# A four-layer graph network on one core: the first layer in two stages with four sets of rows, the second layer's additions behind the next block's weights

## The chip, the cores and the metric

The kernel runs on one core of one Trainium2 chip. The metric is device time in microseconds (us) of one execution, as the median of several; lower is better. Engines are named as the profile names them: PE is TensorE (matmuls; PEld its weight loads), DVE is VectorE, ACT is ScalarE, POOL is GpSimd, SP is SyncE.

## The reference

6250 nodes with 128 features pass through four layers on one graph. After each layer comes `x = layernorm(x + layer(x))`. The edges are 50,000 random pairs in both directions and one loop per node, 106,250 in all, sorted by destination. Only the first two layers matter here:

```python
# layer 0: attention, 4 heads of 32
xp = (x @ W).reshape(n, HEADS, OUT_C)
e = a_src[src] + a_dst[dst]                 # per edge and head
e = where(e >= 0, e, 0.2 * e)
m = segment_max(e, dst)
ex = exp(e - m[dst])
out = segment_sum(ex * xp[src], dst) / segment_sum(ex, dst) + bias
return relu(out)

# layer 1: weighted differences
theta = x[dst] - x[src]
w = sigmoid(relu(theta @ W1 + b1) @ W2 + b2)
agg = segment_sum(w * theta, dst)
return agg + indeg * (x @ W4 + b4)
```

Both have the same shape of work: for each edge, fetch the row of its source (gather), make a weight from source and destination, and add the weighted rows up per destination. The third layer is a linear attention with a graph convolution, the fourth a sum over neighbours with two dense layers.

## The kernel before, in words

**Tiles.** The nodes are cut into NB = 50 blocks of BN = 125. The edges that end in one block fill at most P = 128 partitions x CE = 18 slots, in order of destination. `dl` holds each slot's destination within its block, `e_all` its source row. FEW = 2 blocks make a pair; some work is done once per pair.

**Order.** The program is written as loops in Python; a scheduler then gives each engine its own order of instructions, with semaphores between engines, and pools of buffers (`bufs=3`: three sets) decide when a buffer may be filled again. Where the source wants a fixed order on one engine without a wait, it adds a dependency by hand: `in_order(inst, ahead)` puts `inst` behind `ahead`, and `follow(inst, b)` puts it behind the last weight of block `b` (`behind_of[b]`). Each engine works through its own order strictly: an instruction that waits holds up all behind it.

**First layer, `quick_layer0`, per block `b`:**

- GpSimd issues 18 indirect gathers into `rows` (L828), one per slot column, 128 rows of `table` each. `rows` has three sets, so the gathers of a block can start when the block three earlier has been summed.
- SP loads `dr`, the destinations of all slots broadcast over 125 partitions; VectorE compares it with the lane number (L844), which makes it a one-hot matrix. With it, 18 bf16 matmuls (L848) fetch each slot's destination terms, `pieces`, into `own_ps`.
- VectorE makes the one-hot `m` of 128 x 2250 in one instruction (L851, 2.5 us).
- The maximum per destination: `side` and `off` (L856 to L861), `each` and `top` (within a partition), `sh_ps` (L870: small shifted matmuls that carry maxima over neighbouring partitions), then `near`, `carry`, `far`, `top`, `z` (L873 to L889).
- The exponent (L891, ScalarE), its copy into `rows` (L892), and the product of all rows with it (L896, VectorE, 2.55 us).
- `gathered` (L341): 18 products `m` x `rows` in float32, 36 matmuls in the trace, summed in one PSUM tile. When this sum is done, `rows` and `m` are free.
- One block later, `to_acc` copies the sum into `acc` (L819, ScalarE). After the second block of a pair, `finish` (L783 to L811) divides, adds the bias and the residual, `norm_few` (L360 to L370) normalizes into `X`, and `table1` (L917 to L929) makes and stores the pair's rows for the next layer.
- In between lie the counting of edges per pair of blocks (`count`) and `sort_keys`, in the first 18 pairs and at blocks 0 and 8. They serve the later layers.

After the loop two copies take the columns `indeg` and `selfs` out of `acc`.

**Second layer, `quick_layer1`, per block `b`:**

- 18 gathers (L1012) into one of the three sets `rows_of`: for each edge the source's `x @ W1` and its `x`.
- `dr` as above (L1016, L1017); 54 bf16 matmuls (L1025) lay the destination's `x @ W1 + b1`, split into three bf16 `parts`, out per slot in five PSUM tiles `theta`; VectorE subtracts the gathered part (L1026) and makes relu times `W2`, summed (`junk`, L1029).
- `gw`, the sigmoid (L1039, ScalarE), and `mw`, the one-hot with the weight in it: 18 instructions on VectorE (L1042), one set.
- `gathered` (L341): `mw` x the rows' `x` part.
- `own` for block `b + 2` (L960 to L981: its `x @ W1 + b1` as `y`, L974, and its three `parts`; L975 and L976 its share of the result), `turned` for block `b + 3`.
- The addition of the sum to the block's `acc` (L1051). After the second block of a pair, `finish` (L984 to L1003): the layer's result, its statistics and `X` (`norm_few`), `xs` and its store into `table2`, four matmuls of the pair's Gram matrix (`gram_ps`, L1000 and L1002) and the addition of that to `gram` (L1003).

Of the kernel before, what the change touches and what calls it, by code (L numbers as in the profile page):

```python
# [8 lines left out]
F32 = mybir.dt.float32  # L9
# [28 lines left out]
FEW = 2  # L38
# [13 lines left out]
def kernel(ctx: ExitStack, tc: tile.TileContext, a: dict, out: bass.AP):  # L52
# [87 lines left out]
    def flat(t):  # L140
        return t.rearrange("p b f -> p (b f)")
# [585 lines left out]
    def quick_layer0(table):  # L727
        with tc.tile_pool(name="q0", bufs=1) as st, tc.tile_pool(name="q0w", bufs=2) as wk:
# [16 lines left out]
            load_xp(0)  # L745
            acc = st.tile([BN, NB, W0], F32, name="acc")
            nth = st.tile([P, NB, GP], BF16, name="nth")
# [35 lines left out]
            def finish(b0):  # L783
                sl = slice(b0, b0 + FEW)
                own = wk.tile([BN, 2, FEW, HEADS], F32, name="own")
                nc.vector.tensor_tensor(own[:, 0], xp[:, sl, A0:A0 + HEADS], xp[:, sl, M0:M0 + HEADS], op=ALU.add)
                nc.vector.tensor_tensor(own[:, 1], acc[:, sl, M0:M0 + HEADS], xp[:, sl, M0:M0 + HEADS], op=ALU.add)
# [12 lines left out]
                nc.vector.tensor_tensor(r, r, acc[:, sl, :F], op=ALU.add)  # L800
                rden = wk.tile([BN, FEW, HEADS], F32, name="rden")
                nc.vector.tensor_tensor(rden, acc[:, sl, A0:A0 + HEADS], part, op=ALU.add)
                nc.vector.reciprocal(rden, rden)
                nc.vector.tensor_tensor(r.rearrange("p b (h c) -> p (b h) c", h=HEADS),
                                        r.rearrange("p b (h c) -> p (b h) c", h=HEADS),
                                        rden.rearrange("p b h -> p (b h)")[:, :, None].to_broadcast([BN, FEW * HEADS, OC]),
                                        op=ALU.mult)
                nc.vector.tensor_tensor(r, r, bias[:, None, :].to_broadcast([BN, FEW, F]), op=ALU.add)
                nc.vector.scalar_tensor_tensor(flat(r), flat(r), 0.0, flat(X[:, sl, :]), op0=ALU.max, op1=ALU.add)
                norm_few(wk, b0, r, FEW)  # L810
                table1(ps, wk, w1, b0, r)  # L811

            with tc.tile_pool(name="q0_ps", bufs=2, space=PSUM) as ps:
                node_ps = ps.tile([P, BN], F32, name="node_ps", bufs=1)
                nc.scalar.copy(node_ps, node)
                left_over = []

                def to_acc(b, s):
                    nc.scalar.copy(acc[:, b, :], s)  # L819
                    if b % FEW == FEW - 1:  # L820
                        finish(b - FEW + 1)

                for b in range(NB):
                    rows = wk.tile([P, CE, W0], F32, name="rows", bufs=3)
                    nc.scalar.copy(rows[:, :, TW], ones[:, :CE])
                    nc.scalar.copy(rows[:, :, TW + 1], self_e[:, b, :])
                    for g in range(CE):
                        nc.gpsimd.indirect_dma_start(  # L828
                            out=rows[:, g, :TW], out_offset=None, in_=table,
                            in_offset=bass.IndirectOffsetOnAxis(ap=e_all[:, b, g:g + 1], axis=0))  # L830
                    d = dl[:, b, :]

                    dr = wk.tile([BN, P * CE], BF16, name="dr")
                    row_load = nc.sync.dma_start(dr, dl_rows[b // BPE][b % BPE:b % BPE + 1, :].to_broadcast([BN, P * CE]))
# [7 lines left out]
                    if b % 2 and b // 2 + 1 < NB // BPE:  # L842
                        split_terms(b // 2 + 1)
                    nc.vector.tensor_scalar(dr, dr, lane[:BN], None, op0=ALU.is_equal)  # L844
                    dr_g = dr.rearrange("d (p g) -> d g p", g=CE)
                    own_ps = ps.tile([P, CE, 6 * HEADS], F32, name="own_ps", bufs=1)
                    for g in range(CE):
                        nc.tensor.matmul(own_ps[:, g, :], dr_g[:, g, :], pieces[:, b].rearrange("p q s -> p (q s)"),  # L848
                                         start=True, stop=True)
                    m = wk.tile([P, CE, BN], F32, name="m")  # L850
                    nc.vector.tensor_tensor(m, node_ps[:, None, :].to_broadcast([P, CE, BN]),  # L851
                                            d[:, :, None].to_broadcast([P, CE, BN]), op=ALU.is_equal)

                    off = wk.tile([P, CE, CE], F32, name="off", bufs=1)
                    side = ps.tile([P, 1 + 2 * HEADS, CE], F32, name="side", bufs=1)
                    nc.scalar.copy(side[:, 0, :], d)  # L856
# [12 lines left out]
                    for k in range(2 * SPAN):  # L869
                        nc.tensor.matmul(sh_ps[:, k, :], shift[:, k, :], top[:, :, CE - 1] if k < SPAN else top[:, :, 0],  # L870
                                         start=True, stop=True)
                    own = wk.tile([P, 2 * HEADS, CE], F32, name="own")
                    nc.vector.tensor_reduce(own, own_ps.rearrange("p g (q s) -> p q g s", s=3), axis=AX.X, op=ALU.add)  # L873
# [17 lines left out]
                    nc.scalar.activation(ex, z[:, 0].rearrange("p h g -> p g h"), AF.Exp)  # L891
                    nc.scalar.copy(rows[:, :, A0:A0 + HEADS], ex)  # L892
                    nc.vector.tensor_tensor(rows[:, :, M0:M0 + HEADS].rearrange("p g h -> p h g"), top,
                                            begin[:, b, None, :].to_broadcast([P, HEADS, CE]), op=ALU.mult)
                    msg = rows[:, :, :F].rearrange("p g (h c) -> p g h c", h=HEADS)
                    nc.vector.tensor_tensor(msg, msg, ex[:, :, :, None].to_broadcast([P, CE, HEADS, OC]), op=ALU.mult)  # L896
                    s = gathered(ps, m, rows, W0)
                    for later in left_over:
                        later()
                    left_over = []  # L900
                    if b == 2 * EARLY:
# [3 lines left out]
                        nc.vector.memset(before[0:1, :, 0, :], 0.0)  # L905
                    left_over.append(lambda b=b, s=s: to_acc(b, s))
                    if b == 0:
# [3 lines left out]
                    if b % 2 and b // 2 < EARLY:  # L911
                        left_over.append(count(ps, wk, nth, b // 2))
                for later in left_over:
                    later()
            nc.vector.tensor_copy(indeg, acc[:, :, W0 - 2])
            nc.vector.tensor_copy(selfs, acc[:, :, W0 - 1])

# [13 lines left out]
    def quick_layer1(split=None, besides=None):  # L931

        with tc.tile_pool(name="q1", bufs=1) as st, tc.tile_pool(name="q1w", bufs=2) as wk:
# [11 lines left out]
            with tc.tile_pool(name="q1_ps", bufs=1, space=PSUM) as ps:  # L945
# [18 lines left out]
                def own(b, after):  # L964
# [17 lines left out]
                    y_of[b] = parts  # L982

                def finish(c):  # L984
                    r = acc_of.pop(c)
# [9 lines left out]
                    if split is not None:  # L995
                        split(wk, c * FEW, xs)

                    g_ps = ps.tile([F, F + 1], F32, name="gram_ps")
                    for b in range(c * FEW, (c + 1) * FEW):
                        nc.tensor.matmul(g_ps[:, :F], X[:, b, :], X[:, b, :], start=(b == c * FEW), stop=(b == c * FEW + FEW - 1))  # L1000
                    for b in range(c * FEW, (c + 1) * FEW):
                        nc.tensor.matmul(g_ps[:, F:], X[:, b, :], ones[:BN, 0:1], start=(b == c * FEW), stop=(b == c * FEW + FEW - 1))  # L1002
                    nc.vector.tensor_tensor(gram, gram, g_ps, op=ALU.add)  # L1003

# [4 lines left out]
                for b in range(NB):  # L1009
# [31 lines left out]
                    for g in range(CE):  # L1041
                        last = nc.vector.tensor_scalar(mw[:, g, :], node, dl[:, b, g:g + 1], gw[:, g:g + 1],  # L1042
                                                       op0=ALU.is_equal, op1=ALU.mult)
# [658 lines left out]
```

## Time and profile before

| What | Value |
|---|---|
| Median of 9 runs | 4471.13 us (4433.99 to 4502.01) |
| Profiled execution: its own time | 4439.78 us |
| Its span | 4438.0 us, 46396 instructions |
| Mean granted TensorE clock | 0.7 of full speed |
| PE busy (PEld beside it) | 2439.5 us, 55% (1972.2 us) |
| DVE busy | 2181.1 us, 49% |
| ACT busy | 950.5 us, 21% |
| POOL busy | 2329.9 us, 52% |
| First layer, first to last block | 84 to 1484 us of the span |
| Second layer | 1484 to 3101 us |
| Third and fourth layer | 3101 to 4438 us |

How to read it. The page's slices cut the span in 40 equal parts and give each engine's busy share in tenths. Its groups put together the instructions of one line, engine and shape: count, busy time, the mean of one in ns, and then the idle time of the engine just ahead of them, with what ended it (`<-PE gathered L341`: it ended when that matmul reported; `<-issue`: the engine waited for nothing that the profile shows; `<-remote`: a semaphore whose sender was not found, a DMA among others). The timeline gives instructions in order of time: start, duration, engine, line, operation, and in square brackets the idle time ahead. A table by stretch gives each engine's busy time and number of instructions between two moments.

### The profile page before, as it was taken

Reading aid. Unit: us, or ns where it says so; the run is one execution under the profiler, and the core shown is the slowest. Engines: PE = TensorE matmul, PEld = TensorE weight load, DVE = VectorE, ACT = ScalarE, POOL = GpSimd, SP = SyncE. Lnnn points to the kernel's source line nnn. Section 1 sums busy time; section 2 is a strip of 40 time slices with the busy share of each in tenths; the row PEclk is TensorE's granted clock in tenths of the full one; section 3 lists DMA queues with packets and bytes.
Section 4 is the critical chain, followed back from the end, with each engine's and each line's share of the span. In section 5 each row is a group of like instructions: output and inputs, shape, how many; then the busy total and the mean of one; then the engine's idle time right before and its main releaser. Section 6 shows DMA issues by size and latency. Waiting matters only on the chain.

```text
span 4438.0 us, 46396 instructions
## 1 busy us (share of the span) xinstructions
PE 2439.5 (55%) x16000; PEld 1972.2 (44%) x16000; DVE 2181.1 (49%) x6589; ACT 950.5 (21%) x2088; POOL 2329.9 (52%) x2342
## 2 busy tenths in 40 slices
PE   2255554444444344444444444444578778878877
PEld 2244444444443243434334443434467657734434
DVE  2465555555545444444444444545557667722324
ACT  1011111111111101111111111112344435522224
POOL 4566566666666455565555555553733423075550
PEclk6566566656665566666666666666789989988888
DMA  4442233333332233333333333332323223254441
GB/s 108 93 93 71 68 72 77 78 78 75 76 75 61 79 100 91 97 99 91 96 94 98 89 97 95 98 91 58 96 95 108 99 92 114 108 186 157 156 142 51
DMA packets 187556, 422.00 MB, mean 95 GB/s; under 512 B 52793, under 2 KB 98869, under 8 KB 187301
## 3 DMA queue, kind: packets, MB, share of 16 engines
q0 software_dynamic: 88960, 214.29, 19.9%
q1 hardware_dynamic: 82026, 171.37, 11.1%
q10 hardware_dynamic: 16314, 33.19, 2.1%
q8 instruction: 129, 2.11, 0.2%
q14 instruction: 127, 1.03, 0.1%
HBM read 341.45 MB, written 77.23 MB: 94 GB/s over the span
## 4 chain that ended last, share of the span: by engine, by line
PE 30%; issue 19%; DVE 11%; another core or an unknown queue 4%; ACT 2%; POOL 1%; DMA 1%; DVEq 0%; ACTq 0%; SPq 0%; POOLq 0%
PE acc_ps L1517 7%; PE theta L1025 6%; PE gathered L341 6%; PE acc_ps L1290 3%; DVE mw L1042 3%; DVE hit_d L1273 1%; PE c_ps L1279 1%; DVE load L1220 1%; PE own_ps L972 1%; PE s_ps L1478 1%; DVE hit_s L1270 1%; DVE to L1215 1%; DVE m L1562 1%; PE p L1361 1%
## 5 line engine op out<-in xcount | busy, mean ns | idle before, releaser
L1012 POOL DMA_INDIRECT rows<-table1q,e_all x900 | 875.8, 973 | 698.6 <-PE gathered L341 477.5
L828 POOL DMA_INDIRECT rows<-table0q,e_all x900 | 875.5, 973 | 474.9 <-issue 259.3
L1025 PE MATMUL theta<-parts,dr 125*128 125x128 bf16 x2700 | 347.2, 284 | 524.8 <-issue 521.5
L1025 PEld LDWEIGHTS <-dr 125*128 125x128 bf16 x2700 | 284.9, 156 | 593.4 <-issue 586.6
L341 PE MATMUL gathered<-rows,m 128*125 128x138 f32 x1800 | 357.7, 372 | 259.8 <-DVE rows L896 136.7
L1554 POOL DMA_INDIRECT rows<-table2q,e_all x252 | 284.8, 1130 | 385.9 <-PE pre_ps L1380 246.1
L341 PEld LDWEIGHTS gathered<-rows,m 128*125 128x125 f32 x1800 | 335.3, 270 | 269.8 <-DVE rows L896 143.6
L1554 POOL DMA_INDIRECT rows<-table3q,e_all x252 | 267.2, 1060 | 324.5 <-ACT x L1120 154.0
L1290 PE MATMUL acc_ps<-cs,x 125*128 125x250 bf16 x2700 | 395.1, 280 | 17.2 <-issue 17.1
L341 PE MATMUL gathered<-rows,mw 128*125 128x129 f32 x1800 | 303.5, 345 | 159.4 <-DVE mw L1042 139.4
L1517 PE MATMUL acc_ps<-cs,x 125*128 125x500 bf16 x1350 | 329.4, 396 | 88.8 <-issue 72.5
L341 PEld LDWEIGHTS gathered<-rows,mw 128*125 128x125 f32 x1800 | 294.6, 257 | 164.9 <-DVE mw L1042 141.7
L1280 ACT CAST cs<-c_ps 128x500 bf16<-128x500 f32 x450 | 255.6, 577 | 223.4 <-PE c_ps L1279 131.8
L1290 PEld LDWEIGHTS <-x 125*128 125x128 bf16 x2700 | 270.8, 101 | 66.6 <-issue 25.5
L1042 DVE TENSOR_SCALAR mw<-node,dl,gw 128x125 f32<-128x125 f32 x900 | 249.1, 356 | 54.9 <-issue 52.0
L851 DVE TENSOR_TENSOR m<-node_ps,dl 128x2250 f32<-128x2250 f32 x50 | 125.1, 2501 | 293.7 <-remote 172.3
L1517 PEld LDWEIGHTS <-x 125*128 125x128 bf16 x1350 | 134.0, 100 | 277.6 <-issue 146.5
L1279 PE MATMUL c_ps<-hit_d,hit_s 128*128 128x250 bf16 x900 | 185.6, 285 | 104.4 <-issue 72.5
L1029 DVE SCALAR_TENSOR_TENSOR junk<-theta,W 128x128 f32<-128x128 f32 x900 | 209.1, 286 | 2.9 <-DVE junk L1029 2.9
L848 PE MATMUL own_ps<-pieces,dr 125*128 125x24 bf16 x900 | 62.3, 214 | 233.6 <-DVE own L873 118.2
L870 PE MATMUL sh_ps<-top,shift 128*128 128x4 f32 x600 | 103.8, 278 | 140.8 <-issue 111.9
L1003 DVE TENSOR_TENSOR gram<-gram,gram_ps 128x129 f32<-128x129 f32 x25 | 7.3, 292 | 345.6 <-PE gram_ps L1002 345.6
(364 smaller groups left out, 4007.0 us busy)
## 6 DMA issues: line engine op xcount, KB each, us to landing
dr<-dl_rows SPq DMA_DIRECT2D x100, 562.5 KB
counts<-cs SPq DMA_DIRECT2D x90, 625.0 KB
cs<-counts SPq DMA_DIRECT2D x45, 625.0 KB
cs<-counts ACTq DMA_DIRECT2D x45, 625.0 KB
rows<-table0q,e_all POOLq DMA_INDIRECT x900
rows<-table1q,e_all POOLq DMA_INDIRECT x900
rows<-table2q,e_all POOLq DMA_INDIRECT x252
rows<-table3q,e_all POOLq DMA_INDIRECT x252
```

The costliest lines, as they stand in the source:

```text
L341: nc.tensor.matmul(s, m[:, g, :], rows[:, g, :], start=(g == last_first[0]), stop=(g == last_first[-1]))
L828: nc.gpsimd.indirect_dma_start(out=rows[:, g, :TW], out_offset=None, in_=table, in_offset=bass.IndirectOffsetOnAxis(ap=e_all[:, b, g:g + 1 ...
L851: nc.vector.tensor_tensor(m, node_ps[:, None, :].to_broadcast([P, CE, BN]), d[:, :, None].to_broadcast([P, CE, BN]), op=ALU.is_equal)
L1012: nc.gpsimd.indirect_dma_start(out=rows[:, g, :2 * F], out_offset=None, in_=table1_q, in_offset=bass.IndirectOffsetOnAxis(ap=e_all[:, b, g ...
L1025: nc.tensor.matmul(t[:, j, :], dr_g[:, g0 + j, :], y[:, k, :], start=(k == 0), stop=(k == 2))
L1029: nc.vector.scalar_tensor_tensor(junk, t[:, j, :], 0.0, w2, op0=ALU.max, op1=ALU.mult, accum_out=dot[:, g0 + j:g0 + j + 1])
L1042: last = nc.vector.tensor_scalar(mw[:, g, :], node, dl[:, b, g:g + 1], gw[:, g:g + 1], op0=ALU.is_equal, op1=ALU.mult)
L1279: nc.tensor.matmul(c_ps[:, i, :], hit_s[:, j, :, i], hit_d[:, j, :, i], start=True, stop=True)
L1280: nc.scalar.copy(cs[:, 2 * j:2 * j + 2, :], c_ps)
L1290: nc.tensor.matmul(acc_of[q], x3[:, k * SC + j, i, :], cs[:BN, j, :], start=(k == 0 and j == 0 and i == 0), stop=(k == NB // SC - 1 and j ...
L1517: nc.tensor.matmul(acc[:, :n, :], x3[:, k * SC + j, i, :], cs[:BN, :n, j, :], start=(k == 0 and j == 0 and i == 0), stop=False)
L1554: nc.gpsimd.indirect_dma_start(out=rows[:, g, :], out_offset=None, in_=table, in_offset=bass.IndirectOffsetOnAxis(ap=late_e[:, i, g:g + 1] ...
```

## The change

In the first layer the body of the loop is cut in functions: `gather` (rows, `dr`), `highest` (own terms, maxima, shifted maxima), `weigh` (`m`, weights, the product and the sum) and `step` (what was left over from the block before). The loop now issues `gather(b)`, then `weigh` and `step` of block `b - 1`, then `highest(b)`. `rows` has four sets, `dr` three, `own_ps` and `off` two; `side` gets two places in one PSUM bank that it shares with `node_ps`. The tile `acc` of all 50 blocks is replaced by small ones for a pair (three sets), so that `finish` takes it as an argument and copies `indeg` and `selfs` for each pair. The copy of a sum into `acc` is put, on ScalarE, behind the next block's copy of the exponents.

In the second layer the addition of block `b - 1`'s sum (`add_up`), and with it `finish`, is issued behind the weights of block `b` and ahead of block `b`'s sum. The Gram matmuls of a pair stay in `finish`; the addition of their result to `gram` is kept open until the next pair's `finish` (`add_gram`), and the last one is made after the loop.

```diff
-            acc = st.tile([BN, NB, W0], F32, name="acc")
...
-            def finish(b0):
+            def finish(b0, acc):
...
+                nc.vector.tensor_copy(indeg[:, sl], acc[:, :, W0 - 2])
+                nc.vector.tensor_copy(selfs[:, sl], acc[:, :, W0 - 1])
                 norm_few(wk, b0, r, FEW)
                 table1(ps, wk, w1, b0, r)
...
-                node_ps = ps.tile([P, BN], F32, name="node_ps", bufs=1)
+                n_side = (1 + 2 * HEADS) * CE
+                bank = ps.tile([P, 4 * P], F32, name="bank", bufs=1)
+                node_ps = bank[:, :BN]
+                side_of = [bank[:, BN + k * n_side:BN + (k + 1) * n_side].rearrange("p (h g) -> p h g", g=CE) for k in range(2)]
...
-                def to_acc(b, s):
-                    nc.scalar.copy(acc[:, b, :], s)
+                acc_of, weighed = {}, {}
+
+                def to_acc(b, s, after):
+                    if b % FEW == 0:
+                        acc_of[b // FEW] = wk.tile([BN, FEW, W0], F32, name="acc", bufs=3)
+                    copied = nc.scalar.copy(acc_of[b // FEW][:, b % FEW, :], s)
+                    if after in weighed:
+                        tc.add_manual_dep(copied.ins, weighed[after].ins.name, mybir.DependencyInfo(
+                            mybir.DependencyClass.NoSync, mybir.DependencyReason.DATA), reason="order")
                     if b % FEW == FEW - 1:
-                        finish(b - FEW + 1)
-
-                for b in range(NB):
-                    rows = wk.tile([P, CE, W0], F32, name="rows", bufs=3)
+                        finish(b - FEW + 1, acc_of.pop(b // FEW))
+
+                def gather(b):
+
+                    rows = wk.tile([P, CE, W0], F32, name="rows", bufs=4)
...
-                    dr = wk.tile([BN, P * CE], BF16, name="dr")
+                    dr = wk.tile([BN, P * CE], BF16, name="dr", bufs=3)
...
+                    return rows, dr
+
+                def highest(b, rows, dr):
+
                     nc.vector.tensor_scalar(dr, dr, lane[:BN], None, op0=ALU.is_equal)
...
-                    own_ps = ps.tile([P, CE, 6 * HEADS], F32, name="own_ps", bufs=1)
+                    own_ps = ps.tile([P, CE, 6 * HEADS], F32, name="own_ps")
...
-                    m = wk.tile([P, CE, BN], F32, name="m")
-                    nc.vector.tensor_tensor(m, node_ps[:, None, :].to_broadcast([P, CE, BN]),
-                                            d[:, :, None].to_broadcast([P, CE, BN]), op=ALU.is_equal)
-
-                    off = wk.tile([P, CE, CE], F32, name="off", bufs=1)
-                    side = ps.tile([P, 1 + 2 * HEADS, CE], F32, name="side", bufs=1)
+                    d = dl[:, b, :]
+                    off = wk.tile([P, CE, CE], F32, name="off")
+                    side = side_of[b % 2]
...
+                    return b, rows, own_ps, off, top, sh_ps
+
+                def weigh(b, rows, own_ps, off, top, sh_ps):
+
+                    d = dl[:, b, :]
+                    side = side_of[b % 2]
+                    az = side[:, 1:1 + HEADS, :]
+                    m = wk.tile([P, CE, BN], F32, name="m")
+                    nc.vector.tensor_tensor(m, node_ps[:, None, :].to_broadcast([P, CE, BN]),
+                                            d[:, :, None].to_broadcast([P, CE, BN]), op=ALU.is_equal)
                     own = wk.tile([P, 2 * HEADS, CE], F32, name="own")
...
-                    nc.scalar.copy(rows[:, :, A0:A0 + HEADS], ex)
+                    weighed[b] = nc.scalar.copy(rows[:, :, A0:A0 + HEADS], ex)
...
-                    s = gathered(ps, m, rows, W0)
+                    return gathered(ps, m, rows, W0)
+
+                def step(b, s):
...
-                    left_over.append(lambda b=b, s=s: to_acc(b, s))
+                    left_over.append(lambda: to_acc(b, s, b + 1))
...
+                behind = None
+                for b in range(NB):
+                    rows, dr = gather(b)
+                    if behind is not None:
+                        step(b - 1, weigh(*behind))
+                    behind = highest(b, rows, dr)
+                step(NB - 1, weigh(*behind))
...
-            nc.vector.tensor_copy(indeg, acc[:, :, W0 - 2])
-            nc.vector.tensor_copy(selfs, acc[:, :, W0 - 1])
...
+                open_gram = []
+
+                def add_gram(after=None):
+                    if open_gram:
+                        add = nc.vector.tensor_tensor(gram, gram, open_gram.pop(), op=ALU.add)
+                        if after is not None:
+                            follow(add, after)
+
                 def finish(c):
...
+                    add_gram(2 * c + 2)
                     g_ps = ps.tile([F, F + 1], F32, name="gram_ps")
...
-                    nc.vector.tensor_tensor(gram, gram, g_ps, op=ALU.add)
+                    open_gram.append(g_ps)
+
+                def add_up(b, s, after):
+
+                    at = acc_of[b // FEW][:, b % FEW, :]
+                    follow(nc.vector.tensor_tensor(at, at, s, op=ALU.add), after)
+                    if b % FEW == FEW - 1:
+                        finish(b // FEW)
...
                     behind_of[b] = last
+                    if b:
+                        add_up(b - 1, s, b)
                     s = gathered(ps, mw, rows[:, :, F:], F + 1)
...
-                    at = acc_of[b // FEW][:, b % FEW, :]
-                    nc.vector.tensor_tensor(at, at, s, op=ALU.add)
-                    if b % FEW == FEW - 1:
-                        finish(b // FEW)
+                add_up(NB - 1, s, NB)
+                add_gram()
```

More of the change, by code (lines that the diff above doesn't have):

```diff
@@ L786, in finish @@
                 nc.vector.tensor_tensor(own[:, 0], xp[:, sl, A0:A0 + HEADS], xp[:, sl, M0:M0 + HEADS], op=ALU.add)
-                nc.vector.tensor_tensor(own[:, 1], acc[:, sl, M0:M0 + HEADS], xp[:, sl, M0:M0 + HEADS], op=ALU.add)
+                nc.vector.tensor_tensor(own[:, 1], acc[:, :, M0:M0 + HEADS], xp[:, sl, M0:M0 + HEADS], op=ALU.add)
                 own_f = own.rearrange("p k b h -> p (k b h)")
@@ L799, in finish @@
                                             part[:, j, :, None].to_broadcast(shape[:1] + shape[2:]), op=ALU.mult)
-                nc.vector.tensor_tensor(r, r, acc[:, sl, :F], op=ALU.add)
+                nc.vector.tensor_tensor(r, r, acc[:, :, :F], op=ALU.add)
                 rden = wk.tile([BN, FEW, HEADS], F32, name="rden")
-                nc.vector.tensor_tensor(rden, acc[:, sl, A0:A0 + HEADS], part, op=ALU.add)
+                nc.vector.tensor_tensor(rden, acc[:, :, A0:A0 + HEADS], part, op=ALU.add)
                 nc.vector.reciprocal(rden, rden)
@@ L830, in quick_layer0 @@
                             in_offset=bass.IndirectOffsetOnAxis(ap=e_all[:, b, g:g + 1], axis=0))
-                    d = dl[:, b, :]
-                    dr = wk.tile([BN, P * CE], BF16, name="dr")
+                    dr = wk.tile([BN, P * CE], BF16, name="dr", bufs=3)
                     row_load = nc.sync.dma_start(dr, dl_rows[b // BPE][b % BPE:b % BPE + 1, :].to_broadcast([BN, P * CE]))
@@ L896, in quick_layer0 @@
                     nc.vector.tensor_tensor(msg, msg, ex[:, :, :, None].to_broadcast([P, CE, HEADS, OC]), op=ALU.mult)
-                    s = gathered(ps, m, rows, W0)
+                    return gathered(ps, m, rows, W0)
+                def step(b, s):
+                    nonlocal left_over
                     for later in left_over:
```

## The prediction

> **What bounds the kernel now.** I read the page's slices first: up to slice 28 (about 3100 us) no engine is busy much over 60%, so two stages of waits are in question, not a full engine. The groups of instructions by line then name the two that the change touches: the gathers of the first layer (L828) and the second layer's sum of `gram` (L1003).
>
> ```profile
> L1012 POOL DMA_INDIRECT rows<-table1q,e_all x900 | 875.8, 973 | 698.6 <-PE gathered L341 477.5
> L828 POOL DMA_INDIRECT rows<-table0q,e_all x900 | 875.5, 973 | 474.9 <-issue 259.3
> ...
> L1003 DVE TENSOR_TENSOR gram<-gram,gram_ps 128x129 f32<-128x129 f32 x25 | 7.3, 292 | 345.6 <-PE gram_ps L1002 345.6
> ```
>
> L1003 costs 0.29 us a time, and VectorE stands 345.6 / 25 = 13.8 us before each. GpSimd issues a gather in 0.95 us and the next 0.30 us later, so 18 gathers (a **stream**, one block) last 22.5 us.
>
> Both layers show one behaviour that decides this case. Busy time by stretch, cut where streams begin and where TensorE slows; behind the stretch and its length stand busy us and (x instructions) of PE, PEld, DVE, ACT, POOL, then clock and DMA:
>
> ```profile
> 2202.80:2217.10 14.30, 9.79 (x68) 9.04 (x67) 8.46 (x50) 1.18 (x4) 10.95 (x12) 0.75 0.33 93
> 2217.10:2228.30 11.20, 1.53 (x6) 0.84 (x6) 5.45 (x18) 0.00 (x0) 6.37 (x7) 0.64 0.33 94
> 2231.10:2243.30 12.20, 8.83 (x68) 8.47 (x68) 6.00 (x35) 1.85 (x3) 9.46 (x10) 0.78 0.56 144
> 2243.30:2256.50 13.20, 1.72 (x7) 0.72 (x6) 0.48 (x6) 3.35 (x7) 7.59 (x9) 0.50 0.32 90
> ...
> 920.80:937.60 16.80, 9.34 (x67) 9.13 (x67) 11.66 (x30) 1.52 (x8) 12.79 (x14) 0.52 0.39 87
> 937.60:946.10 8.50, 2.11 (x7) 1.22 (x5) 3.36 (x7) 0.00 (x0) 4.47 (x5) 0.66 0.53 114
> ```
>
> After a stream's start TensorE issues about 67 matmuls, whatever they are, and then **crawls**: 6 or 7 in 8 to 13 us, until some 4 us behind the stream's last gather. VectorE goes on at a reduced pace (18 in 11.2 us, 0.62 us each). Why, the trace does not say; I use it as a rule of this kernel.
>
> What TensorE has issued is also reported late. The first layer, in order of time:
>
> ```profile
> 906.41 6.03 PE L341 MATMUL gathered<-rows,m 128*125 128x138 f32 x36 [4.81 <-DVE rows L896]
> ...
> 916.35 0.95 POOL L828 DMA_INDIRECT rows<-table0q,e_all  x1 [0.30 <-issue]
> ...
> 920.62 0.28 ACT L819 COPY acc<-gathered 125x138 f32<-125x138 f32 x1 [13.19 <-PE sh_ps L870]
> 920.62 2.50 DVE L851 TENSOR_TENSOR m<-node_ps,dl 128x2250 f32<-128x2250 f32 x1 [9.99 <-PE sh_ps L870]
> ...
> 920.85 0.95 POOL L828 DMA_INDIRECT rows<-table0q,e_all  x1 [3.55 <-remote]
> ```
>
> The sum of a block is issued by 912.44, and its three readers start together at 920.6, when the stream that ended at 917.3 is 3.3 us past. The freed rows then start the next stream. So a first-layer block lasts 22.5 + 3.3 = 25.8 us, and the gap is made by the stream itself, not by missing buffers. The second layer, an odd block:
>
> ```profile
> 2246.32 0.31 ACT L1039 ACTIVATE gw<-dot,b 128x18 f32<-128x18 f32 x1
> ...
> 2256.59 1.70 PE L1025 MATMUL theta<-parts,dr 125*128 125x128 bf16 x14 [0.45 <-issue]
> ...
> 2260.25 0.29 DVE L1003 TENSOR_TENSOR gram<-gram,gram_ps 128x129 f32<-128x129 f32 x1 [15.70 <-PE gram_ps L1002]
> ...
> 2262.40 3.40 DVE L1042 TENSOR_SCALAR mw<-node,dl,gw 128x125 f32<-128x125 f32 x13
> ...
> 2265.86 1.44 PE L341 MATMUL gathered<-rows,mw 128*125 128x129 f32 x5 [5.64 <-DVE mw L1042]
> ```
>
> The weights' input `gw` is there at 2246.6, but L1003 stands ahead of the 18 weights of L1042 and waits for matmuls that are behind the crawl. Only then come the weights (5.3 us to 2265.8), the block's sum, and the stream that follows it 1.06 us later. Streams start at 2202.8, 2231.1 and 2266.9: 28.3 us for an even block, 35.8 for an odd one, 64.1 a pair.
>
> **Second layer, part by part.** The wait of L1003 goes, since the sum of one pair is added a pair later. The addition of L1051 (0.29 us, waits for its block's sum; 248.3 us idle ahead of it in all, 45 times) moves behind the next block's weights. Late next is the end of the theta matmuls: crawl ends at 2256.6, they last 1.7 us, so the next sum can start at 2258.3 in place of 2265.9, and an odd block falls towards the 28.3 us of an even one, where the weights are already done in the crawl.
>
> New costs there. The gram matmuls (2257.98 to 2260.2, 2.2 us) move into the middle of the next block's sum; they spend 8 of that stream's 67 matmuls, so 8 theta matmuls more wait for the crawl's end (8 x 0.11 = 0.9 us). Between 0.9 and 2.2 us, I take 1.6: nearer neither, so the middle. They wait in TensorE's queue for ScalarE's `X` (L370); behind them stand the rest of the sum, theta, and through the sum's rows GpSimd. `X` needs statistics that now follow the weights in the crawl, and the new `y` (L974) stands ahead of the second of them, waiting for matmuls held to its end; some 3.5 to 4 us later `X` is there, when 8 to 10 of the sum's 18 slices (0.22 to 0.43 us each) have run: 0 to 0.5 us, taken 0. The weights now start when the last block's sum is reported (11.1 us after its start: 2201.7 to 2212.85 at L1051), or 2 us later with gram in it; 18 x 0.62 = 11.2 us, done 24.5 us after the start: hidden by theta's end at 28.3. If that cover goes, each weight is 0.2 to 0.6 us on the path. The new wait of the sum for the addition adds one 0.29 us instruction ahead of it, in the same cover. `xs` to `table2` and its DMA come half a pair later, read by nothing in this stage. So a pair is 28.3 + 28.3 + 1.6 = 58.2, 5.9 us less, and 24 of the 25 sums have a block behind them: **-142 us** (bounds: 24 x 7.6 = -182, all of 35.8 - 28.3 and no cost; 0, if the crawl takes it back).
>
> The moved weights now run beside gathers. The even blocks show the price: the gathers issued at 2216.75 to 2224.33, beside L1042, last 0.95 to 1.00 us at the same spacing; so none. The Trainium skill, "SBUF — State Buffer", section "Who interferes with whom", speaks against this: a `tensor_scalar` of VectorE can take the port pair that GpSimd needs to write descriptors, and block it for the whole instruction. By that rule 18 weights of 0.35 us would add up to 6.3 us to a stream; these rows do not show it.
>
> **First layer, part by part.** A fourth set of rows lets a stream start one block sooner. It does not take away the gap: with the sets full, a stream still starts when a block's sum is reported, and in that stream TensorE has the same work as now (18 own, 36 gathered, 12 shifted matmuls, 4 to 8 of table 1: about 70 a block, over its 67). The program as built keeps VectorE's order too, a block's weights ahead of the next block's maxima; only L851 moves ahead of the shifted maxima. Its 2.5 us now lie in the held time: worth 0 while the hold lasts. `dr` in three buffers, two of `own_ps`, `side` and `off`: 0, for the same reason (L844's waits for its DMA, 49.6 us in the layer, lie in it). The two copies of `indeg` and `selfs` per pair (0.16 us each, by the 125-row rows L787 and L791) lie in VectorE's idle time; 50 x 0.16 = 8 us if not. ACT's ordered copy of `acc` waits for weights' instructions just ahead of it in its queue: 0.
>
> The tail gains: the last three sums run free of gathers, 1437.4 to 1453.6 is 16.2 us a block, against 25.8; now one block more does: -9.6. The head loses: the first sum (167.5 to 174.4) now falls under the fourth set's stream, which ends near 175, and is reported up to 3.5 us behind it: +4. Of the slow early blocks (174 to 611, 29 us each, with counting and sorting) I take nothing. Sum **-6**, bounds -165 (the gap of 3.3 us gone in 50 blocks) and +225 (below).
>
> **Sum.** -142 - 6 = -148 us on the profiled execution's 4439.8 (span 4438.0): 4292. It lies 31 us under the median of 9 runs, 4471.1; the same 148 from there gives **4323**. Layers three and four (3101 to 4438) are untouched.
>
> **Rivals.** *The fourth set does what its size suggests*: sums are reported inside the stream and the gap goes in some 45 blocks, 3.3 x 45 = 149 more: 4323 - 149 = 4174. For it: GpSimd's wait is 80.7 us "remote" alone between 600 and 1434. Against: 917.3 to 920.6 above. It would need the sum reported before the stream's last gather.
>
> *Slower: streams back to back.* If a sum is just reported in time, the next stream starts with no gap, TensorE's 67 are spent, and it crawls through that whole stream; then GpSimd waits for a block done free of gathers. Two blocks then take 2 x 22.5 + 3.5 + some 13 (a free 16.2 less what was issued) = 61.5, against 51.6: +5 a block, +225 in 45. With the second layer's gain: 4323 + 6 + 225 = 4554. It decides where own plus gathered, 54 matmuls, are reported within 22.5 us of a stream's start; against it, the block from 946.6 to 972.3 issued about as many and had to wait.
>
> *The second layer gives nothing back*: `X` or the weights, late in the crawl, take the place of the gram wait, and a pair stays near 64: 4455 to 4480. For it: the crawl ends with the stream whatever VectorE does. Against: even blocks already do it in 28.3.
>
> **Chances.** Forecast 0.61, its own range 4270 to 4400 (second layer -90 to -182, first layer -20 to +20); gap gone 0.12; back to back 0.13; nothing gained 0.14. 0.5%, some 22 us, is about what can be told from no change: faster 0.78 (forecast, gap gone, a part of the last), same 0.09, slower 0.13. Range 4170 to 4460: it leaves out the slower rival and the upper end of the last.
>
> **What would show it.** Right: L1003's wait near 0; the second layer's streams 28 to 30 us apart in both kinds of blocks; the first layer's still 25.8 with 3.3 us gaps; a last row in the first layer with 4 free blocks. Wrong: gaps under 0.5 us at every stream (first rival), streams joined two by two and then a wait of over 10 us (second), L341's wait for L1042 still 5 us in odd blocks (third).

## The result, and the profile after

The changed kernel takes 4280.94 us (median of 10 runs, 4266.11 to 4346.03), the kernel before 4470.09 us beside it (31 runs). The ratio is **0.9584**, 95% interval 0.9558 to 0.961: about 190 us less. (The ratio leaves out the slowest executions, so it differs a little from that of the medians.) The forecast was 4323, with a range of 4170 to 4460. The profiled execution of the changed kernel has a span of 4262.0 us against 4438.0, 176 us less. By stage, cut at the first gather of each layer:

| Stage | Before, us | After, us | Difference | Forecast |
|---|---|---|---|---|
| First layer | 1399.1 | 1433.1 | +34.0 | -6 |
| Second layer | 1619.7 | 1425.1 | -194.6 | -142 |
| Third and fourth | 1334.8 | 1318.9 | -15.9 | 0 |

So the total came out near the forecast with one term too small and another of the wrong sign; that the two errors nearly cancel is luck. The code of the third and fourth layer is the same; runs of one kernel lie up to 70 us apart (4432 to 4502), so those 16 us are not read further.

The profile's groups of the two gathers, and below them the answer for the line of the `gram` addition (now L1019):

```profile
L1059 POOL DMA_INDIRECT rows<-table1q,e_all x900 | 877.5, 975 | 505.8 <-PE gathered L341 226.9
L840 POOL DMA_INDIRECT rows<-table0q,e_all x900 | 874.6, 972 | 495.7 <-issue 259.1
```

```profile
L1019 DVE TENSOR_TENSOR gram<-gram,gram_ps x25: 255/259/291, 1713.2 to 2939.9; 128x129 f32<-128x129 f32 x25
its engine sat idle before it (us, times) until:
  PE gram_ps L1042: 1.8, 1
```

The wait ahead of the addition fell from 345.6 us to 1.8, that of the sums' addition (now L1048) to 6.0. GpSimd's idle time ahead of the second layer's gathers fell by 193 us, as much as the stage; that ahead of the first layer's rose by 21.

**A block with the Gram matmuls, and one without.** Busy time by stretch in the second layer (columns as in the table of the prediction):

```profile
2157.40:2163.80 6.40, 6.40 (x51) 6.29 (x50) 6.20 (x38) 2.49 (x7) 4.82 (x6) 0.81 0.64 157
2163.80:2174.90 11.10, 0.03 (x1) 0.00 (x0) 0.82 (x1) 0.18 (x2) 6.89 (x7) 0.63 0.40 118
2174.90:2181.80 6.90, 5.74 (x47) 5.24 (x47) 4.86 (x20) 1.98 (x4) 5.36 (x6) 0.61 0.30 80
2184.00:2201.90 17.90, 6.71 (x56) 5.97 (x54) 10.18 (x53) 0.67 (x3) 13.58 (x15) 0.68 0.47 128
2201.90:2212.60 10.70, 4.03 (x28) 3.66 (x29) 5.16 (x27) 2.21 (x5) 3.74 (x4) 0.50 0.22 63
```

The last two rows are a block without a new pause: TensorE issues 56 matmuls, crawls, and the next stream starts 28.6 us after this one (2184.0 to 2212.6). The first three rows are new. TensorE issues 51 matmuls and stands, waiting for `xt`; then it goes on at 2174.9, with six gathers still to come, and the block lasts 26.5 us. The timeline shows what let it go:

```profile
2171.57 0.95 POOL L1059 DMA_INDIRECT rows<-table1q,e_all  x1 [0.30 <-issue]
2174.72 0.27 ACT L993 COPY xt<-own_ps 128x125 f32<-128x125 f32 x1 [14.29 <-remote]
...
2174.92 0.95 POOL L1059 DMA_INDIRECT rows<-table1q,e_all  x1 [2.40 <-remote]
...
2175.04 1.22 PE L1003 MATMUL own_ps<-w,xt 128*125 128x256 f32 x2 [11.20 <-ACT xt L993]
...
2176.05 4.72 PE L1072 MATMUL theta<-parts,dr 125*128 125x128 bf16 x45
...
2176.60 0.31 ACT L1086 ACTIVATE gw<-dot,b 128x18 f32<-128x18 f32 x1
2176.95 4.68 DVE L1089 TENSOR_SCALAR mw<-node,dl,gw 128x125 f32<-128x125 f32 x18 [12.06 <-ACT gw L1086]
...
2181.53 0.29 DVE L1048 TENSOR_TENSOR acc<-acc,gathered 125x129 f32<-125x129 f32 x1
...
2181.88 0.59 PE L341 MATMUL gathered<-rows,mw 128*125 128x129 f32 x3 [1.10 <-issue]
```

The 13th gather waits 2.40 us, and TensorE, ScalarE and GpSimd all start within 0.4 us of 2174.7, 2.2 us behind the end of the 12th gather. In the program's order for TensorE the Gram matmuls begin behind the 12th slice of the sum. The slices behind them are issued by 2163.2, but their reports come late, in ones and twos, while gathers go on; the trace's semaphore records have the last of them at 2174.6. In each steady stream of this kind 13 gathers carry a wait for TensorE; in the other steady streams, and in those of the kernel before, 12 do. The 13th gather is due at 2172.8, finds the sum not fully reported and stops the stream; the pause then does what the end of a stream did: it lets everything go. **The stream splits itself, and the crawl's release comes six gathers earlier.**

One execution holds its own comparison. Of the streams 8 to 47, counted from 0, 16 have such a pause and last 26.5 to 26.7 us; 24 have none and last 27.9 to 28.7. The odd-numbered streams are those with the Gram matmuls: 15 have the pause and last 26.58 us on average, 5 do not and last 28.47 (one of these stops for 0.6 us and gains nothing); the even ones without it last 28.33. What decides is when the report comes: `xt`, whose matmul stands just behind the sum, starts 1.7 to 2.3 us behind the moment at which the 13th gather is due in the 15 streams, and from 1.3 us ahead of it to 0.4 us behind it in the 5. (In the kernel before, the long streams, 35.6 us, were the even-numbered ones; the prediction names them odd blocks, after the block whose `finish` falls in them.)

**The first layer** loses in its first third. The moment at which a block's sum frees its rows (seen as the start of the stream that waits for it) is later than before by 12.3 us for block 0, 39.6 for block 15, 46.2 for block 45; the last sum's copy is 34.5 later. So: head +12, blocks 1 to 15 (with the counting) +27, 30 steady blocks +7 (26.05 a block against 25.83), tail -12.

### The profile page after: what moved, and what is told of

Read it like the earlier page. It is cut to its first block, busy times and chain, and to the rows that moved or that the text cites. A ratio compares the mean times of both kernels' runs of the same rounds, so it can differ in the third digit from the quotient of the medians.

```text
span 4262.0 us, 46620 instructions
## 1 busy us (share of the span) xinstructions
PE 2345.4 (55%) x16000; PEld 1908.6 (45%) x16000; DVE 2183.3 (51%) x6637; ACT 937.9 (22%) x2088; POOL 2332.6 (55%) x2342
## 4 chain that ended last, share of the span: by engine, by line
another core or an unknown queue 18%; DVE 18%; PE 17%; issue 6%; ACT 4%; POOL 1%; DMA 0%; DVEq 0%; ACTq 0%; POOLq 0%
PE acc_ps L1564 7%; DVE mw L1089 5%; PE acc_ps L1337 3%; DVE junk L1076 2%; DVE hit_d L1320 1%; DVE theta L1073 1%; POOL rows L1059 1%; DVE load L1267 1%; PE c_ps L1326 1%; PE s_ps L1525 1%; DVE hit_s L1317 1%; DVE to L1262 1%; DVE m L1609 1%; ACT L1086 1%
## 5 line engine op out<-in xcount | busy, mean ns | idle before, releaser
L1072 PE MATMUL theta<-parts,dr 125*128 125x128 bf16 x2700 | 310.1, 287 | 282.9 <-issue 263.7
L341 PE MATMUL gathered<-rows,m 128*125 128x138 f32 x1800 | 338.0, 361 | 174.1 <-DVE rows L917 92.8
L1089 DVE TENSOR_SCALAR mw<-node,dl,gw 128x125 f32<-128x125 f32 x900 | 235.7, 368 | 361.7 <-ACT gw L1086 262.1
L341 PEld LDWEIGHTS gathered<-rows,m 128*125 128x125 f32 x1800 | 323.1, 262 | 176.3 <-DVE rows L917 95.9
L1003 PE MATMUL own_ps<-w,xt 128*125 128x256 f32 x100 | 60.2, 703 | 448.7 <-ACT xt L993 322.0
L341 PE MATMUL gathered<-rows,mw 128*125 128x129 f32 x1800 | 264.2, 309 | 32.6 <-issue 22.5
L881 PE MATMUL sh_ps<-top,shift 128*128 128x4 f32 x600 | 123.3, 317 | 264.2 <-DVE top L878 126.1
L341 PEld LDWEIGHTS gathered<-rows,mw 128*125 128x125 f32 x1800 | 250.3, 221 | 38.6 <-issue 28.2
L881 PEld LDWEIGHTS sh_ps<-top,shift 128*128 128x128 f32 x600 | 124.2, 296 | 276.3 <-issue 272.4
L1003 PEld LDWEIGHTS own_ps<-w,xt 128*125 128x125 f32 x100 | 24.6, 307 | 455.3 <-ACT xt L993 326.5
```

Of the source, the lines that this page charges most:

```text
L341: nc.tensor.matmul(s, m[:, g, :], rows[:, g, :], start=(g == last_first[0]), stop=(g == last_first[-1]))
L1072: nc.tensor.matmul(t[:, j, :], dr_g[:, g0 + j, :], y[:, k, :], start=(k == 0), stop=(k == 2))
```

## The experiments

**Four parts alone, beside one kernel before.** `e1`: the second layer of the changed kernel with the first of before. `e2`: the other way round (in both, the function of one layer is exchanged whole). `e3`: only the `gram` addition is late:

```diff
+                open_gram = []
+
+                def add_gram():
+                    if open_gram:
+                        nc.vector.tensor_tensor(gram, gram, open_gram.pop(), op=ALU.add)
...
+                    add_gram()
                     g_ps = ps.tile([F, F + 1], F32, name="gram_ps")
...
-                    nc.vector.tensor_tensor(gram, gram, g_ps, op=ALU.add)
+                    open_gram.append(g_ps)
...
+                add_gram()
```

`e4`: `e1`, but the `gram` addition at once, behind its matmuls:

```diff
-                    add_gram(2 * c + 2)
...
                     open_gram.append(g_ps)
+                    add_gram()
```

> The first layer of the kernel before, the second layer of the changed one. Theory (the two layers' shares are what the two traces show: the second layer's stage is 195 us shorter, the first layer's 35 us longer, and they don't touch each other): some 4470 - 195 = 4275 from the median of before, some 20 to 35 us less than the changed kernel (4281 less 35 is 4246, so 4245 to 4275). Rival (the first layer's 35 us are a shift of the boundary between the stages, and the second layer takes them back): the time of the changed kernel, 4281. Second layer's pairs 55 to 57 us in both theories.

> The first layer of the changed kernel, the second layer of the kernel before. Theory (the first layer's change costs: head 12, blocks with counting 28, steady blocks 6, tail -12): 4470 + 35 = 4505, slower than before by 0.5 to 1%. Rival (the prediction's -6 holds and the boundary is shifted): 4464, no difference.

> The kernel before, with nothing changed but that a pair's addition to gram is made at the next pair. The addition of each sum stays where it was. Theory (the wait of the gram addition alone made odd blocks 35.8 us, as the prediction has it): odd blocks near 28.3, a pair 57 to 58.5, without a split stream, so 24 x 6 to 7 us less: 4300 to 4325. Rival (both edits are needed: the sum's addition waits in VectorE's order and delays the weights as well): a pair over 61, 4400 or more.

> First layer of before, second layer of the changed kernel, but the addition to gram is made at once, right behind its matmuls. Theory (the gram matmuls now stand in the middle of the next sum, their report is held until the stream pauses, some 15 us after the stream's start, and VectorE stands for it ahead of the rest of the theta work, about 5 us of it): sums start some 4 to 5 us later in one block of two, a pair 59 to 60, 24 x 4.5 = 108 us over the kernel with the second layer's change alone: 4355 to 4385. Rival (the gram addition's place no longer matters once the sums' additions are moved): no more than 15 us over that kernel.

None of the forecast times came, and theory could not be told from rival, for a reason that none of the four had: on the chip of these runs the kernel **before takes 3486.88 us** (33 runs, 3480.0 to 3493.37), 983 us less than on the chip of the result, and the four variants take 3490.82, 3495.16, 3487.10 and 3485.26. Ratios: 1.0009 (1.0 to 1.0018), 1.0025 (1.0016 to 1.0034), 1.0006 (0.9997 to 1.0015), 1.0002 (0.9993 to 1.0011). Two first-layer blocks and two second-layer blocks of `e3`, each from one stream's start to the next:

```profile
756.90:779.40 22.50, 9.97 (x38) 8.72 (x39) 12.50 (x26) 6.21 (x16) 17.06 (x18) 0.57 0.31 71
779.40:802.20 22.80, 13.21 (x102) 12.63 (x100) 14.62 (x32) 1.70 (x8) 17.27 (x19) 0.75 0.49 107
1758.60:1781.60 23.00, 13.56 (x95) 12.64 (x94) 14.12 (x70) 2.65 (x6) 17.50 (x18) 0.63 0.47 128
1781.60:1804.50 22.90, 13.40 (x104) 12.61 (x103) 14.77 (x74) 5.52 (x14) 17.41 (x18) 0.70 0.49 135
```

There is no crawl: TensorE issues 102, 95 and 104 matmuls beside 18 gathers (38 in the first row; two sums fall into the second), where it crawled behind 67 on the other chip. The gathers follow one another with the same 0.95 and 0.30 us, and a block is 18 of them, 22.5 to 23 us, in both layers and all variants. The waits of additions still stand in the trace and cost nothing: in `e3` L988 waits 41.3 us in all.

**The changed kernel again**, to see whether the parts must act together:

> The changed kernel itself, once more, timed beside the kernel before on one chip. Four parts of the change ran beside a kernel before that took 3487 us, not 4470, and none moved it by more than 0.25%: there TensorE never crawled and GpSimd issued gathers almost without a gap. Theory (the whole gain is time that TensorE loses behind gathers, so it exists only on a chip that shows the crawl): where the kernel before takes about 3487, the ratio is 1.000 to 1.005; where it takes about 4470, it is 0.95 to 0.965 again. Rival (the two parts of the change must act together to gain): 0.96 beside a kernel before of 3487 too, that is about 3340.

It met a chip with the crawl: before 4366.06 us (11 runs), changed 4218.53 (6 runs), ratio 0.968 (0.9637 to 0.9724). So the gain is reproduced where the crawl is (the ratio a little above the 0.95 to 0.965 expected), with the same split streams: 26.4 us on average with a pause, 27.9 without. The changed kernel as a whole was not run on a chip without the crawl, so the rival is not excluded by a run; it has no mechanism in these traces.

**The parts once more**, with `e5`: `e1`, but with the Gram matmuls put behind the last matmul of the next sum:

```diff
+                        mm = nc.tensor.matmul(g_ps[:, :F], X[:, b, :], X[:, b, :], start=(b == c * FEW), stop=(b == c * FEW + FEW - 1))
+                        if behind is not None:
+                            in_order(mm, behind)
...
                     s = gathered(ps, mw, rows[:, :, F:], F + 1)
+                    if b and b % FEW == 0:
+                        gram_of(b // FEW - 1, last_of[-1])
```

> First layer of before, second layer of the changed kernel, once more, for a chip with the crawl. Theory (the layers' shares as the two traces show them, -195 and +35): 0.950 to 0.962 of before, 20 to 40 us below the changed kernel; pairs of the second layer 55 to 57 us. Rival (the first layer's 35 us are a shifted boundary): the changed kernel's own ratio, 0.958 to 0.968. On a chip without the crawl both say 1.000.

> First layer of the changed kernel, second layer of before, once more, for a chip with the crawl. Theory (head 12, blocks with counting 28, steady blocks 6, tail -12): slower by 25 to 40 us, 1.006 to 1.010. Rival (the prediction's -6 was right): 0.998 to 1.000.

> The kernel before with the addition to gram made at the next pair and nothing else, once more, for a chip with the crawl. Theory (the wait of the gram addition alone made odd blocks 35.8 us): odd blocks near 28.3, a pair 57 to 58.5, 145 to 170 us less, 0.961 to 0.968. Rival (the sums' additions have to move too): a pair over 61, 0.985 or more.

> First layer of before, second layer of the changed kernel, but the pair's gram matmuls are put behind the next block's whole sum, in TensorE's order, and not between its 12th and 13th slice. Theory (in the changed kernel the slices behind the gram matmuls are reported only when the stream has paused, so the stream splits into 12 and 6 gathers, TensorE is let go in the pause, and such a block lasts 26.5 us instead of 28.5): without the split both blocks are 28.3 to 28.5, plus 0.9 for eight more matmuls at the crawl's end; a pair 57 to 58, 24 x 2 to 3 = 48 to 70 us over the kernel with the second layer's change alone. Rival (the split stream is a side effect and costs or gives nothing): the time of that kernel, within 15 us, a pair of 55 to 56.

A second chip without the crawl: before 3487.71 us, and 1.0007 (0.9998 to 1.0017), 1.0024 (1.0015 to 1.0033), 1.0001 (0.9992 to 1.001), 1.0004 (0.9995 to 1.0013). Nothing is told of the split. One thing repeats: the changed first layer is slower by 0.24 to 0.25% (the medians differ by 8.3 us on the one chip, 6.5 on the other), the changed second layer is not faster.

**A fourth buffer for `dr`, and the late `gram` addition**, in one kernel, to be read by stage:

```diff
-                    dr = wk.tile([BN, P * CE], BF16, name="dr", bufs=3)
+                    dr = wk.tile([BN, P * CE], BF16, name="dr", bufs=4)
```

> Two questions in one kernel, read from its two stages. First layer: that of the changed kernel with a fourth buffer for dr. Second layer: that of before, but the addition to gram is made at the next pair (the sums' additions stay). On a chip with the crawl. Second layer, theory (the wait of the gram addition alone made odd blocks 35.8 us): odd blocks near 28.3, a pair 57 to 58.5; rival (the sums' additions have to move too): a pair over 61. First layer, theory (the 28 us lost in the blocks with counting are VectorE waiting for dr, whose load stands behind a held report: 39.3 us of such waits against 7.4): with one more buffer the stage is 20 us or more shorter than the 1417 to 1433 us of the changed kernel, near 1400; rival (the longer chain from a block's maxima to its sum costs it): 1415 to 1435. On a chip without the crawl: blocks of 22.7 to 23.0 us in both layers, and nothing can be told.

> The same kernel as the run before it, once more, for a chip with the crawl: first layer of the changed kernel with a fourth buffer for dr, second layer of before with the addition to gram made at the next pair. Theory: a pair of the second layer 57 to 58.5 us, odd blocks near 28.3, and a first layer near 1400 us. Rivals: a pair over 61; a first layer of 1415 to 1435. Without the crawl: blocks of 22.7 to 23.0 us again.

Two more chips, again without the crawl: 3499.77 beside 3490.39 (1.0027, 1.0015 to 1.0038) and 3493.98 beside 3489.5 (1.0013, 1.0003 to 1.0023). In the first of them a first-layer block is 22.9 us, a pair of the second layer 45.95. Both questions stay open. Both kernels hold the changed first layer, and both are slower by a little, as it was alone.

**Half of the gathers** of the first layer, with a plain load in place of the others and the second layer of `e3`; it says something on either kind of chip:

```diff
+                    nc.sync.dma_start(rows[:, CE // 2:, :TW], table[:P * CE // 2].rearrange("(p g) f -> p g f", p=P))
-                    for g in range(CE):
+                    for g in range(CE // 2):
                         nc.gpsimd.indirect_dma_start(
```

> The kernel before with the addition to gram made at the next pair, and in the first layer 9 of a block's 18 gathers left out: one plain load of as many bytes on SP's queue stands in for them (rows of other nodes, so the result is another). First layer, on a chip without the crawl. Theory (there GpSimd's issue of 18 gathers, 22.5 us, bounds each block, which is why no variant moves it): a block of 9 gathers, 11.3 us, falls to what the other engines need, VectorE's 13.5 us busy at least and the 16.2 us of a block free of gathers at most: 14 to 17 us, 50 x 6 to 9 = 300 to 450 us less in all. Rival (the landing of the rows or the chain from maxima to sum bounds it): blocks of 20 us or more, less than 150 us. On a chip with the crawl. Theory (the gap is made by the stream, 22.5 + 3.3): 11.3 + 3.3 = 14.6 us of stream and gap, fewer matmuls in the crawl, a block of 16 to 18 us. Rival (TensorE's own work behind the crawl sets it): over 20. Second layer, on such a chip: a pair of 57 to 58.5 us by the theory that the gram addition's wait alone made odd blocks long, over 61 by the rival; without the crawl 46 us.

A chip without the crawl: 3359.05 us beside 3491.44, ratio 0.962 (0.9604 to 0.9636), 132 us less. The theory fell in its size: a steady block takes 18.8 us, neither 14 to 17 nor over 20. GpSimd's part of the timeline, the first gather of two blocks in turn:

```profile
812.57 0.94 POOL L829 DMA_INDIRECT rows<-table0q,e_all  x1 [10.06 <-PE gathered L341]
...
828.98 0.94 POOL L829 DMA_INDIRECT rows<-table0q,e_all  x1 [5.44 <-PE gathered L341]
```

GpSimd now waits for sums, 16.4 us from one block to the next (812.57 to 828.98), then about 21.1 in the block where a pair is finished. So the gathers do bound a steady block there, but the next bound lies only 4 us below. In the blocks with counting they do not: blocks 4 to 18 take 22.7 us each with 9 gathers, 23.1 in `e3` with 18. The rival's sum (under 150 us) held, its reason did not in the steady blocks.

## Why the prediction was right, and where it was not

**The total** is right in part by luck. The second layer gave 53 us more than forecast, the first took 40 us more, and the two errors cancel but for 13. Neither layer lies in the range that the forecast gave it (second -90 to -182, first -20 to +20).

**What bounded the kernel** was read rightly for the chip of the traces: the wait of L1003 went, and the long streams (the odd blocks of the prediction) fell from 35.6 to 28.3 us, an even block's time, as forecast (28.3). That the wait of the `gram` addition alone would have done it was not shown: on a chip with the crawl, only the whole change ran.

**The Gram matmuls' cost of 1.6 us a pair** was the mis-sized term. An odd-numbered stream, which holds them, takes 28.47 us where it does not split, an even one 28.33: 0.1 us. Where it splits, it gains 1.9 us. Over the streams 8 to 47 a pair takes 55.29 us, not 58.2, and 63.82 before: 20 pairs save 171 us where 20 x 5.9 = 118 were forecast, and those 53 us are what -195 exceeds -142 by. The bound of -182, all of the wait and no cost, was passed too, since it had no place for a gain. The working had TensorE's order right (the matmuls in the middle of the sum) and the hold of reports right, and did not put the two together: it did not ask what the 13th gather waits for. The wait for `X`, taken at 0, was 0: `X` is done at 2158.5, the Gram matmuls start at 2160.68.

**The cover of the weights** (theta's end) is gone in the split blocks. In the timeline above the path runs from the release over the sigmoid's input, `gw`, the 18 weights (4.68 us, 0.26 each) and the addition to the sum at 2181.88; the theta matmuls end at 2180.8. The prediction named that price, 0.2 to 0.6 us a weight, for the case that the cover goes.

**The ports.** The gathers beside the moved weights last 0.94 to 1.04 us (2176.17 to 2181.29) against 0.95: 0.1 us more in all five together. Over the whole layer the 216 gathers that overlap a moved weight last 0.976 us on average, the other 684 last 0.975. That agrees with the row from before, and not with a stream longer by 6.3 us as the rule of the Trainium skill ("SBUF — State Buffer", section "Who interferes with whom") would have it if these instructions took the shared ports.

**The first layer's gap** stayed, as forecast: the stream that ends at 933.7 is followed by one at 937.2. Neither the first rival (gap gone, 4174) nor the slower one (streams joined, 4554) came. The tail gained 12 us where 9.6 were forecast. **The head** was mis-sized, 12 for 4. The release was taken as 3.5 us behind the stream's end; behind four sets, 72 gathers without a break up to 176.4, TensorE's own part of the timeline still crawls at 186:

```profile
181.46 0.29 PE L862 MATMUL own_ps<-pieces,dr 125*128 125x24 bf16 x2 [2.51 <-DVE low L1131]
184.22 0.18 PE L862 MATMUL own_ps<-pieces,dr 125*128 125x24 bf16 x1 [2.47 <-issue]
185.63 0.18 PE L862 MATMUL own_ps<-pieces,dr 125*128 125x24 bf16 x1 [1.24 <-issue]
186.33 1.04 PE L862 MATMUL own_ps<-pieces,dr 125*128 125x24 bf16 x14 [0.52 <-issue]
```

**"Of the slow early blocks I take nothing"** is the step that failed: they lost 27 us. The change moves the preparation of a block past the counting of the one before, and these blocks were never bound by gathers alone. VectorE's waits in that part, first the changed kernel (186 to 650 us), then the kernel before (174 to 611):

```profile
DVE dr L858 <- DMA dr<-dl_rows: 39.3, 8, 11.5
DVE near L896 <- PE sh_ps L881: 28.8, 8, 9.9
DVE off L868 <- ACT bank L867: 28.7, 5, 9.9
```

```profile
DVE own L873 <- remote: 46.0, 5, 14.5
...
DVE dr L844 <- issue: 12.1, 3, 4.7
...
DVE dr L844 <- DMA dr<-dl_rows: 7.4, 4, 3.9
```

The columns are us in all, times, and the longest. VectorE waits for the load of `dr` 39.3 us, against 7.4; that the load itself stands behind a held report is inferred. "`dr` in three buffers: 0" is where that would belong. But it was only argued. Other waits shrank: that for `own`, 46.0 us before, comes to 14.4; all of VectorE's waits in this part come to 219 us, 194 before. The run with a fourth buffer met no chip with the crawl, and which of these waits makes the 27 us stays open.

**The rule itself** (67 matmuls, then the crawl) carried the forecast on the chip of the profile, and is not a rule of this kernel, as the prediction called it: the same instructions do not show it on four other chips. Nor is 67 a fixed count: in the stream of the changed kernel that does not split, shown above, the crawl follows some 55.

## What to carry to other kernels

An addition that waits for a late result belongs behind the work that waits for nothing, since everything behind it on its engine pays; here 13.8 us of wait stood ahead of weights that were ready. Before a large stall without a known cause is tuned around, the same kernel should be timed on another chip: this change is worth 3 to 4% where the stall is; where it is not, its second half alone gives nothing and its first half alone costs 0.25%. And a fourth set of buffers did not help here, where the report that would free a set comes only behind the stream that fills one.

## What the runs showed of the hardware

The crawl belongs to the chip or its condition, not to the program. The runs of the result have it (before: 4470 us) and those of the repeated run (4366 us; whether on the same chip is not recorded); four other chips do not (3487 to 3491 us, all within 0.2%). The first layer, with the same code, takes 1183 us in `e3` there and 1399 in the kernel before on the first chip, the second (in `e3` with the late addition) 1176 and 1620, the third and fourth 1056 and 1335, with the granted clock at 0.97 in these last two on the one chip and 0.87 on the other. The spacing of the gathers is the same on both, 1.25 us. What makes TensorE and VectorE slow down behind gathers on some chips no run varied; it stays open.
